# A graph network with attention on one core: shorter timetables for the attention of the last four pairs

## Chip, core and metric

The kernel runs on one core of a Trainium2 chip. The metric is the device time of one launch in microseconds (us): the median over several executions of the same program. The profile comes from one more execution; its span, from the first to the last instruction, is a little shorter than the timed figure.

## What is computed

There are 64 graphs of N = 256 nodes with D = 256 features each. A gated graph network (three layers, one GRU cell shared by all) is followed by one graph attention layer; each has a residual sum and a layer norm. Cut to what matters:

```python
A = (adj != 0)
h = x
for i in range(3):                       # gated graph network
    m = h @ weight[i]
    aggr = A^T @ m                       # over the nodes
    h = gru(aggr, h)                     # r, z sigmoid; n tanh; (1 - z) * n + z * h
v = layernorm(x + h)

wh = v @ W                               # attention
e = leaky_relu(s1[:, None] + s2[None, :])   # s1 = wh @ a1, s2 = wh @ a2
attn = softmax(where(adj > 0, e, -9e15))
out = layernorm(v + attn @ wh)
```

## The kernel before

**Tiling.** Two graphs make a pair, so 32 pairs (NP = 32) are worked off, numbered 0 to 31. A pair has K = 4 groups of 128 nodes; a tile of 128 partitions by 512 columns holds one half of the features of all its nodes, and fills one PSUM bank. The pool `psum` has eight banks; a product, a transpose or a projection takes the one that has been free for longest and waits until its last reader is done.

**Precision.** The products of the GRU split each operand in an upper part, a remainder and a difference (`pieces`, `upper`, `lower`, `cross`; H, L and D in the names), so that a gate product with a hidden and an input part is twelve passes of 128 by 512, one with a single part six. They are collected in two banks: `pga` (H and L parts) and `pgb` (D parts).

**Blocks.** Layer i of pair p is a block (p, i). The list `blocks` interleaves three pairs at different layers: it ends ... (31,0), (30,1), (29,2), (31,1), (30,2), (31,2). Each block is one call of `gates`, which issues the eight gate products of the two feature halves e = 0 and 1 (r, n, z, t each). After every six passes `product` calls `tick()`.

**The clock.** `tick()` advances a counter, and issues every step that is due. Everything else than the gate products hangs on that counter: `at(t, step)` puts a step into a heap, `run_due` takes out those whose time has come. A block has 12 ticks. So the instruction order of all five engines is written by this timetable at build time; at run time each engine works its own queue off in order, and waits by semaphore for the others.

**What hangs on it.** `front(p, i, t, pace)` prepares the next block (transposes `from_T`, splits, aggregation) in the ticks of the present one, by the tables `CLOSE` or `LOOSE`. In `gates`, the lags (2, 3, 5) or (4, 5, 10) say how many ticks after the last product of a half its tanh, its blend and its update of the state `hT` follow. The blend is done by GpSimd (two operations of 128 by 512, L394 and L395; the sum before the tanh is L404).

**Attention.** When the third block of a pair is done, `attention(p, clock)` puts its steps into the heap, with fixed offsets to that moment: reload the saved input (+5), `join` it with the state (+14), transpose back (+15), evacuate to `v` (+17), statistics of the layer norm (+23), its power and shift (+26, +28), projection by W (+31 to +34, each spread one tick later with the scale of the norm), the score rows (+36), the leaky ReLU (+37), mask (+38), row maximum (+39), exponentials (+46, +47), reciprocal and transposes of the weights (+52, +53), their evacuation (+54), product with `wh` (+57), sum (+58), second layer norm (+61 to +70) and store (+72). So the attention of a pair is spread over six blocks of other pairs. Pair 28 comes to its end about when the last block does. Pairs 29, 30 and 31 begin 36, 12 and 0 ticks before the end of the last block, and what is left of them is issued by the last loop, which has no gate products any more:

```python
    while pending:
        clock[0] = pending[0][0]
        run_due()
```

I call that part the tail. In it the three pairs' steps stand in the queues in the order of their due ticks.

**ScalarE's tables.** Exponentials (`exps`, L507) and sigmoids and tanh (`gate`, L386) need different activation tables, so a table load stands between them wherever the order changes from one kind to the other. In the middle of the kernel the exponentials of a pair stand at ticks 10 and 11 of a block, between the last sigmoid of that block and the first of the next: one load before them and one after.

Of the kernel before, what the change touches and what calls it, by code (L numbers as in the profile page):

```python
# [9 lines left out]
F32 = mybir.dt.float32  # L10
# [15 lines left out]
def kernel(  # L26
# [329 lines left out]
    def gates(p, i, lags):  # L356

        s = pairs[p]

        def product(dst, o, parts, bias=None):  # L360

            a, b = bank("pga"), bank("pgb")
            todo = [(a, w[k], m[k], d) for w, m in parts for k in (0, 1) for d in range(C)]
            ends = len(todo) - 1
            todo += [(b, w[2], m[2], d) for w, m in parts for d in range(C)]
            step = len(todo) // len(parts)
            for n, (pt, w, m, d) in enumerate(todo):
                nc.tensor.matmul(pt, w[:, d, o * P:(o + 1) * P], m[:, d, :],  # L368
                                 start=n in (0, ends + 1), stop=n in (ends, len(todo) - 1))
                if (n + 1) % step == 0 and n + 1 < len(todo):  # L370
                    tick()
            if bias is None:
                nc.scalar.activation(dst, a, AF.Copy, scale=1.0 + U)  # L373
            else:
                nc.scalar.activation(dst, a, AF.Identity, scale=1.0 + U, bias=bias)  # L375
            tick()
            nc.vector.scalar_tensor_tensor(dst, b, -1.0 / U, dst, op0=ALU.mult, op1=ALU.add)  # L377

        for e in range(C):
            nm = f"{p}_{i}_{e}"  # L380

            def temp(tag, bufs=2):
                return work.tile([P, GN], F32, tag=tag, name=f"{tag}_{nm}", bufs=bufs)

            def gate(dst, func, bias):
                nc.scalar.activation(dst, dst, func, bias=bias)  # L386

            hid, inp = (whh, s.hc), (wc[i], s.ag)
            bo = [b_sum[:, e:e + 1], b_sum[:, C + e:C + e + 1]]
            r, n, z, t = temp("r", 1), temp("n", 3), temp("z"), temp("t")  # L390
            h = s.hT[:, e, :]

            def blend(n=n, z=z, t=t, h=h):
                nc.gpsimd.tensor_sub(t, h, n)  # L394
                nc.gpsimd.tensor_mul(t, t, z)  # L395

            product(r, e, [hid, inp])
            after(1, lambda r=r, b=bo[0]: gate(r, AF.Sigmoid, b))
            product(n, 2 * C + e, [hid], bh[:, 2 * C + e:2 * C + e + 1])
            after(2, lambda r=r, n=n: nc.gpsimd.tensor_mul(n, n, r))  # L400
            product(z, C + e, [hid, inp])
            after(2, lambda z=z, b=bo[1]: gate(z, AF.Sigmoid, b))
            product(t, 2 * C + e, [inp])
            after(1, lambda n=n, t=t: nc.gpsimd.tensor_add(n, n, t))  # L404
            after(lags[0], lambda n=n, b=bi[:, 2 * C + e:2 * C + e + 1]: gate(n, AF.Tanh, b))
            after(lags[1], blend)
            after(lags[2], lambda n=n, t=t, h=h: nc.vector.tensor_add(h, t, n))

    def layer_norm(v, name, t, then=None):

        st = work.tile([P, K, nc.vector.BN_STATS_DIM], F32, tag="st_" + name[0], name=f"st_{name}")
        mv = work.tile([P, K, nc.vector.BN_AGGR_DIM], F32, tag="mv_" + name[0], name=f"mv_{name}")
        rs = work.tile([P, K], F32, tag="rs_" + name[0], name=f"rs_{name}")
        nm = work.tile([P, K], F32, tag="nmr_" + name[0], name=f"nmr_{name}")

        def stats(k):
            nc.vector.bn_stats(st[:, k, :], v[:, k // C, k % C, :])  # L417
            nc.vector.bn_aggr(mv[:, k, :], st[:, k, :])

        def power():  # L420
            nc.gpsimd.tensor_scalar(rs, mv[:, :, 1], EPS, None, op0=ALU.add)
            nc.gpsimd.tensor_tensor(rs, rs, half, ALU.pow)

        def shift():
            nc.vector.scalar_tensor_tensor(nm, mv[:, :, 0], -1.0, rs, op0=ALU.mult, op1=ALU.mult)

        def apply(k):
            vk = v[:, k // C, k % C, :]
            nc.scalar.activation(vk, vk, AF.Identity, scale=rs[:, k:k + 1], bias=nm[:, k:k + 1])  # L429

        for k in range(K):
            at(t[0] + k // 2, lambda k=k: stats(k))
        at(t[1], power)
        at(t[2], shift)
        for k in range(K):
            at(t[3] + k // 2, lambda k=k: apply(k))
        if then:
            at(t[3] + 2, then)
        return rs

    def attention(p, t):

        s = pairs[p]
        pts = {}

        def again():
            s.vT = room("vT", [P, C, GN], p)
            nc.sync.dma_start(s.vT, s.far)
        at(t + 5, again)
        at(t + 14, lambda: nc.vector.tensor_add(flat(s.vT), flat(s.vT), flat(s.hT)))  # L450

        def back(d):
            if d == 0:
                s.v = room("v", [P, G, C, D], p)
            pts[d] = from_T(s.vT, d)
        for d in range(C):
            at(t + 15 + d, lambda d=d: back(d))
            at(t + 17 + d, lambda d=d: nc.vector.tensor_copy(
                nodes(s.v, d), pts[d].rearrange("p (k n) -> p k n", k=K)))
        at(t + 18, lambda: setattr(s, "rs", layer_norm(s.v, f"a_{p}", (t + 23, t + 26, t + 28, t + 49))))  # L460

        def project(k):
            if k == 0:
                s.wh = room("wh", [P, G, C, D], p)
                s.s1 = work.tile([P, K], F32, tag="s1", name=f"s1_{p}")
                s.s2 = work.tile([P, K, P], F32, tag="hi0", name=f"s2_{p}", bufs=1)
            pts[k] = bank("pwh")
            for d in range(C):
                nc.tensor.matmul(pts[k][:, :D + 2], s.vT[:, d, k * P:(k + 1) * P], gw[:, d, :],  # L469
                                 start=(d == 0), stop=(d == C - 1))  # L470
# [8 lines left out]
                else:  # L479
                    nc.vector.tensor_scalar(dst, src, rs, None, op0=ALU.mult)  # L480
        for k in range(K):
            at(t + 31 + k, lambda k=k: project(k))
            at(t + 32 + k, lambda k=k: spread(k))

        def rows():
            pts[0] = bank("s2")
# [3 lines left out]
        def scores():  # L490
            s.sc = room("sc", [P, K, N], p)
            for k in range(K):
                nc.scalar.activation(s.sc[:, k, :], pts[0][:, (k // C) * N:(k // C + 1) * N], AF.Prelu,
                                     bias=s.s1[:, k:k + 1], alpha=ALPHA)
        at(t + 36, rows)
        at(t + 37, scores)

        s.nm = work.tile([P, K], F32, tag="nm", name=f"nm_{p}")
        s.sm = work.tile([P, K], F32, tag="sm", name=f"sm_{p}")

        def masked():
            nc.vector.copy_predicated(flat(s.sc), flat(s.mask), neg.to_broadcast([P, K * N]))  # L502
        at(t + 38, masked)
        at(t + 39, lambda: nc.vector.tensor_reduce(s.nm, s.sc, AX.X, ALU.max, negate=True))

        def exps(k):
            nc.scalar.activation(s.sc[:, k, :], s.sc[:, k, :], AF.Exp, bias=s.nm[:, k:k + 1],  # L507
                                 accum_out=s.sm[:, k:k + 1])
        for k in range(K):
            at(t + 46 + k // 2, lambda k=k: exps(k))  # L510
        at(t + 52, lambda: nc.vector.reciprocal(s.sm, s.sm))

        def weights_T(g):
            pts[g] = bank("pt")
# [16 lines left out]
                nc.vector.scalar_tensor_tensor(s.v[:, g, c, :], pts[g][:, c * D:(c + 1) * D], s.sm[:, k:k + 1],  # L531
                                               s.v[:, g, c, :], op0=ALU.mult, op1=ALU.add)
        for g in range(G):
            at(t + 53 + g, lambda g=g: weights_T(g))
            at(t + 54 + g, lambda g=g: nc.vector.tensor_copy(flat(s.sc[:, g * C:(g + 1) * C, :]), pts[g]))
            at(t + 57 + g, lambda g=g: combine(g))
            at(t + 58 + g, lambda g=g: add(g))
# [4 lines left out]
        at(t + 60, lambda: layer_norm(s.v, f"b_{p}", (t + 61, t + 64, t + 66, t + 70), store))  # L542


    CLOSE = (5, 5, 5, 7, 8, 8), (6, 6, 7)
    LOOSE = (2, 3, 4, 6, 7, 8), (5, 8, 10)


    blocks = []
# [28 lines left out]
    for n, (p, i) in enumerate(blocks):  # L578
        if n + 1 < len(blocks):
            np_, ni = blocks[n + 1]  # L580
            if ni == 0:
                after(1, lambda p=np_: begin(p))
            front(np_, ni, clock[0], CLOSE if n and np_ == blocks[n - 1][0] else LOOSE)
            if ni == 0:
                after(7, lambda p=np_: load_x(p + 1))
                after(16, lambda p=np_: masking(p))
                after(17, lambda p=np_: load_adj(p + 1))
        gates(p, i, (2, 3, 5) if n + 2 >= len(blocks) or blocks[n + 2][0] == p else (4, 5, 10))
        if i == L - 1:
            attention(p, clock[0])  # L590
    while pending:
        clock[0] = pending[0][0]
        run_due()
# [29 lines left out]
```

## Time and profile before

| | |
|---|---|
| time, median of 3 | 2256.81 us (2254.84 to 2256.81) |
| span of the profiled execution | 2254.2 us, mean granted TensorE clock 0.991 |
| TensorE (PE) busy | 2205.3 us, 98% |
| VectorE (DVE) busy | 1627.0 us, 72% |
| ScalarE (ACT) busy | 1494.6 us, 66% |
| GpSimd (POOL) busy | 1496.7 us, 66% |
| last gate matmul ends at | 2189.24 us |
| the tail, from there to the end of the span | 65.0 us |

The busy share of TensorE says that nearly the whole span is bound by it. The table's last two rows come from the chain of waits, which ends its list of gate products (L368) at 2188.78 us with a piece of 0.46 us. After it TensorE has work only now and then: the pieces of attention of three pairs, each waiting for the other engines.

### The profile page before, as it was taken

The page shows a single profiled execution, that of the slowest core. Times are in us where ns is not written, and L with a number is a line of the kernel's source. Part 1 is how long each engine was busy: PE and PEld are TensorE (multiplying, and loading weights), DVE is VectorE, ACT ScalarE, POOL GpSimd, SP SyncE. Part 2 cuts the span into 40 slices and gives each one's busy share as a digit, 9 for nine tenths or more (in the row PEclk, how much of TensorE's full clock was granted, in tenths as well). Part 3 has the DMA queues.
Part 4 walks back from the last instruction along what each step waited for, and adds up shares of the span by engine and source line. Part 5 has one row for each costly group of instructions (what it writes and reads, how often), then busy time and mean ns, then how long its engine had stood idle before and what let it go on. Part 6 is the DMA issues. An engine that isn't in the chain of part 4 may idle for free.

```text
span 2254.2 us, 31118 instructions
## 1 busy us (share of the span) xinstructions
PE 2205.3 (98%) x10980; PEld 1839.0 (82%) x10980; DVE 1627.0 (72%) x2856; ACT 1494.6 (66%) x2771; POOL 1496.7 (66%) x1084
## 2 busy tenths in 40 slices
PE   7999999999999999999999999999999999999985
PEld 5788888888888888888888888888888888888874
DVE  4767777777767777767777767777767777767775
ACT  4556667666667666667666677666677666677664
POOL 5777666676666676666667666667666667666661
PEclk9999999999999999999999999999999999999997
DMA  3001011100011101011101011101011101010000
GB/s 112 29 29 38 28 39 48 47 31 36 34 42 48 47 29 38 30 46 47 47 29 37 29 47 47 48 29 38 29 48 47 47 29 38 29 47 29 20 28 28
DMA packets 62650, 88.50 MB, mean 39 GB/s; under 512 B 2784, under 2 KB 54240, under 8 KB 62496
## 3 DMA queue, kind: packets, MB, share of 16 engines
q1 hardware_dynamic: 60704, 84.68, 10.7%
q8 instruction: 87, 1.43, 0.3%
q10 hardware_dynamic: 1616, 1.57, 0.2%
q14 instruction: 67, 0.55, 0.1%
q0 software_dynamic: 176, 0.27, 0.1%
HBM read 52.96 MB, written 33.55 MB: 38 GB/s over the span
## 4 chain that ended last, share of the span: by engine, by line
PE 95%; DVE 1%; ACT 1%; POOL 1%; issue 1%; DMA 1%; SPq 0%; POOLq 0%; ACTq 0%; DVEq 0%
PE pga L368 47%; PE pgb L368 23%; PE pa L339 8%; PE po L525 5%; PE pwh L469 5%; PE pt L274 4%; PE pt L268 1%; PE pt L517 1%; DMA adj<-in_adj_dram 1%; PE s L488 1%; PE pw L229 0%; ACT v L429 0%; DVE sc L502 0%; DVE st_b L417 0%; POOL wc2L_wc L145 0%
## 5 line engine op out<-in xcount | busy, mean ns | idle before, releaser
L394 POOL TENSOR_TENSOR t<-hT,n 128x512 f32<-128x512 f32 x192 | 255.0, 1328 | 534.3 <-ACT n L386 534.2
L368 PE MATMUL pga<-hH,whhH_whh 128*128 128x512 f32 x1152 | 397.4, 426 | 0.0
L368 PE MATMUL pgb<-hD,whhD_whh 128*128 128x512 f32 x1152 | 361.9, 395 | 0.3 <-DVE hD L134 0.3
L368 PE MATMUL pga<-hL,whhL_whh 128*128 128x512 f32 x1152 | 362.0, 395 | 0.0
L404 POOL TENSOR_TENSOR n<-n,t 128x512 f32<-128x512 f32 x192 | 251.8, 1311 | 114.2 <-DVE t L377 101.2
L377 DVE SCALAR_TENSOR_TENSOR r<-pgb,r 128x512 f32<-128x512 f32 x192 | 131.8, 686 | 254.0 <-PE pgb L368 188.5
L400 POOL TENSOR_TENSOR n<-n,r 128x512 f32<-128x512 f32 x192 | 306.2, 1595 | 0.6 <-DVE n L377 0.4
L395 POOL TENSOR_TENSOR t<-t,z 128x512 f32<-128x512 f32 x192 | 263.1, 1370 | 15.0
L368 PEld LDWEIGHTS pgb<-hD,whhD_whh 128*128 128x128 f32 x1152 | 216.3, 188 | 52.6 <-DVE hD L134 0.8
L368 PEld LDWEIGHTS pga<-hL,whhL_whh 128*128 128x128 f32 x1152 | 216.7, 188 | 51.4
L373 ACT ACTIVATE r<-pga 128x512 f32<-128x512 f32 x192 | 115.2, 600 | 216.0 <-PE pga L368 206.2
L375 ACT ACTIVATE n<-pga,bh 128x512 f32<-128x512 f32 x192 | 131.7, 686 | 164.6 <-PE pga L368 164.5
L131 POOL TENSOR_TENSOR hL<-hT,hH 128x1024 fp32r<-128x1024 f32 x96 | 230.6, 2402 | 7.1 <-ACT hH L128 7.1
L368 PEld LDWEIGHTS pga<-hH,whhH_whh 128*128 128x128 f32 x1152 | 193.9, 190 | 20.8
L339 PE MATMUL pa<-A,hi 128*128 128x256 f32 x768 | 200.4, 293 | 0.0
L373 ACT ACTIVATE z<-pga 128x512 f32<-128x512 f32 x192 | 114.7, 597 | 128.7 <-PE pga L368 128.7
L339 PE MATMUL pa<-A,lo 128*128 128x256 f32 x768 | 192.7, 283 | 4.3 <-POOL lo L131 4.3
L377 DVE SCALAR_TENSOR_TENSOR t<-pgb,t 128x512 f32<-128x512 f32 x192 | 131.8, 686 | 78.3 <-ACT t L373 72.3
L377 DVE SCALAR_TENSOR_TENSOR z<-pgb,z 128x512 f32<-128x512 f32 x192 | 131.9, 687 | 73.7 <-ACT z L373 60.9
L131 DVE TENSOR_TENSOR aL<-pa,aH 128x512 fp32r<-128x512 f32 x192 | 131.6, 685 | 55.4 <-ACT aH L128 55.4
L128 ACT ACTIVATE aH<-pa 128x512 fp32r<-128x512 f32 x192 | 115.1, 600 | 78.5 <-PE pa L339 78.5
L377 DVE SCALAR_TENSOR_TENSOR n<-pgb,n 128x512 f32<-128x512 f32 x192 | 131.8, 686 | 43.7 <-ACT n L375 39.3
(133 smaller groups left out, 5439.6 us busy)
## 6 DMA issues: line engine op xcount, KB each, us to landing
x<-in_x_dram SPq DMA_DIRECT2D x32, 512.0 KB, 4.0
adj<-in_adj_dram SPq DMA_DIRECT2D x32, 512.0 KB, 4.0
xT<-hT SPq DMA_DIRECT2D x32, 512.0 KB, 2.6
vT<-xT SPq DMA_DIRECT2D x32, 512.0 KB, 4.8
out_dram<-v SPq DMA_DIRECT2D x32, 512.0 KB, 2.9
w_n<-in_L_gnn_weight_dram ACTq DMA_DIRECT2D x3, 256.0 KB, 10.4
rows_hH<-in_L_gnn_w_hh_dram SPq DMA_DIRECT2D x1, 512.0 KB, 5.5
rows_aH<-in_L_gnn_w_ih_dram ACTq DMA_DIRECT2D x1, 512.0 KB, 6.0
```

The lines of the kernel that those rows point to most:

```text
L128: nc.scalar.activation(dst, src, AF.Copy, scale=1.0 - 2.0 ** -13)
L131: eng.tensor_sub(dst, src, hi.bitcast(F32))
L339: nc.tensor.matmul(pt[:, g * N:(g + 1) * N], h[:, g * C + c, :], s.A[:, g, c, :], start=(n == 0), stop=(n == len(todo) - 1))
L368: nc.tensor.matmul(pt, w[:, d, o * P:(o + 1) * P], m[:, d, :], start=n in (0, ends + 1), stop=n in (ends, len(todo) - 1))
L373: nc.scalar.activation(dst, a, AF.Copy, scale=1.0 + U)
L375: nc.scalar.activation(dst, a, AF.Identity, scale=1.0 + U, bias=bias)
L377: nc.vector.scalar_tensor_tensor(dst, b, -1.0 / U, dst, op0=ALU.mult, op1=ALU.add)
L394: nc.gpsimd.tensor_sub(t, h, n)
L395: nc.gpsimd.tensor_mul(t, t, z)
L400: after(2, lambda r=r, n=n: nc.gpsimd.tensor_mul(n, n, r))
L404: after(1, lambda n=n, t=t: nc.gpsimd.tensor_add(n, n, t))
L469: nc.tensor.matmul(pts[k][:, :D + 2], s.vT[:, d, k * P:(k + 1) * P], gw[:, d, :], start=(d == 0), stop=(d == C - 1))
```

## The change

The offsets become a table that depends on the pair. Pairs 0 to 27 keep theirs (`EVEN`). Pair 28 gets `BRISK` (the second layer norm's application at +54 instead of +70), pairs 29 to 31 get `FAST` (+33). The purpose is that less attention work is left when the gate products end. Three more parts belong to it:

- For these four pairs half of the evacuations of `v` and of the transposed weights move from VectorE to ScalarE (`copy`, even index).
- `s2`, which shared a buffer with the split of the next block (`hi0`), lies for these pairs in the buffer of the input `x`, which is free by then.
- The last block of pairs 29, 30 and 31 uses the short lags (2, 3, 5), and the last half of the last block does its three elementwise operations on VectorE instead of GpSimd.

```diff
+            add_by = nc.vector if (p, i, e) == (NP - 1, L - 1, C - 1) else nc.gpsimd
+
-            def blend(n=n, z=z, t=t, h=h):
-                nc.gpsimd.tensor_sub(t, h, n)
-                nc.gpsimd.tensor_mul(t, t, z)
+            def blend(n=n, z=z, t=t, h=h, eng=add_by):
+                eng.tensor_sub(t, h, n)
+                eng.tensor_mul(t, t, z)
...
-            after(1, lambda n=n, t=t: nc.gpsimd.tensor_add(n, n, t))
+            after(1, lambda n=n, t=t, eng=add_by: eng.tensor_add(n, n, t))
...
-    def attention(p, t):
+    def attention(p, t, pace):
...
+        T = {k: t + dt for k, dt in zip(
+            "again join back v stats power shift apply project rows scores mask max exp turn combine "
+            "stats2 power2 shift2 apply2".split(), pace)}
+
+        def copy(j, dst, src):
+            if pace is EVEN or j % 2:
+                nc.vector.tensor_copy(dst, src)
+            else:
+                nc.scalar.copy(dst, src)
...
-                s.s2 = work.tile([P, K, P], F32, tag="hi0", name=f"s2_{p}", bufs=1)
+                if pace is EVEN:
+                    s.s2 = work.tile([P, K, P], F32, tag="hi0", name=f"s2_{p}", bufs=1)
+                else:
+                    s2 = io.tile([P, G, C, D], F32, tag="x", name=f"s2_{p}")
+                    s.s2 = s2[:, 0].rearrange("p c (h n) -> p (c h) n", n=P)
...
+    EVEN = 5, 14, 15, 17, 23, 26, 28, 49, 31, 36, 37, 38, 39, 46, 53, 57, 61, 64, 66, 70
+    BRISK = 5, 14, 15, 17, 19, 21, 23, 32, 23, 28, 29, 30, 31, 33, 37, 41, 45, 48, 50, 54
+    FAST = 2, 5, 6, 7, 9, 10, 12, 22, 14, 18, 19, 20, 20, 22, 25, 27, 30, 31, 33, 33
...
-        gates(p, i, (2, 3, 5) if n + 2 >= len(blocks) or blocks[n + 2][0] == p else (4, 5, 10))
+        pace = EVEN if p < NP - 4 else BRISK if p < NP - 3 else FAST
+        close = n + 2 < len(blocks) and blocks[n + 2][0] == p or i == L - 1 and pace is FAST
+        gates(p, i, (2, 3, 5) if close else (4, 5, 10))
         if i == L - 1:
-            attention(p, clock[0])
+            attention(p, clock[0], pace)
```

The numbers of each table stand in the order of the names in `T`.

More of the change, by code (lines that the diff above doesn't have):

```diff
@@ L448, in again @@
             nc.sync.dma_start(s.vT, s.far)
-        at(t + 5, again)
-        at(t + 14, lambda: nc.vector.tensor_add(flat(s.vT), flat(s.vT), flat(s.hT)))
+        at(T["again"], again)
+        at(T["join"], lambda: nc.vector.tensor_add(flat(s.vT), flat(s.vT), flat(s.hT)))
         def back(d):
@@ L456, in attention, with norm @@
         for d in range(C):
[L457 to L460, printed above, removed]
+            at(T["back"] + d, lambda d=d: back(d))
+            at(T["v"] + d, lambda d=d: copy(d, nodes(s.v, d), pts[d].rearrange("p (k n) -> p k n", k=K)))
+        def norm():
+            s.rs = layer_norm(s.v, f"a_{p}", [T[k] for k in ("stats", "power", "shift", "apply")])
+        at(T["v"] + 1, norm)
         def project(k):
@@ L481, in attention @@
         for k in range(K):
-            at(t + 31 + k, lambda k=k: project(k))
-            at(t + 32 + k, lambda k=k: spread(k))
+            at(T["project"] + k, lambda k=k: project(k))
+            at(T["project"] + 1 + k, lambda k=k: spread(k))
         def rows():
@@ L494, in scores @@
                                      bias=s.s1[:, k:k + 1], alpha=ALPHA)
-        at(t + 36, rows)
-        at(t + 37, scores)
+        at(T["rows"], rows)
+        at(T["scores"], scores)
         s.nm = work.tile([P, K], F32, tag="nm", name=f"nm_{p}")
@@ L502, in masked @@
             nc.vector.copy_predicated(flat(s.sc), flat(s.mask), neg.to_broadcast([P, K * N]))
-        at(t + 38, masked)
-        at(t + 39, lambda: nc.vector.tensor_reduce(s.nm, s.sc, AX.X, ALU.max, negate=True))
+        at(T["mask"], masked)
+        at(T["max"], lambda: nc.vector.tensor_reduce(s.nm, s.sc, AX.X, ALU.max, negate=True))
         def exps(k):
@@ L509, in attention @@
         for k in range(K):
-            at(t + 46 + k // 2, lambda k=k: exps(k))
-        at(t + 52, lambda: nc.vector.reciprocal(s.sm, s.sm))
+            at(T["exp"] + k // 2, lambda k=k: exps(k))
+        at(T["turn"], lambda: nc.vector.reciprocal(s.sm, s.sm))
         def weights_T(g):
@@ L533, in attention @@
         for g in range(G):
[L534 to L537, printed above, removed]
+            at(T["turn"] + g, lambda g=g: weights_T(g))
+            at(T["turn"] + 1 + g, lambda g=g: copy(g, flat(s.sc[:, g * C:(g + 1) * C, :]), pts[g]))
+            at(T["combine"] + g, lambda g=g: combine(g))
+            at(T["combine"] + 1 + g, lambda g=g: add(g))
         def store():
@@ L541, in store @@
             del pairs[p]
-        at(t + 60, lambda: layer_norm(s.v, f"b_{p}", (t + 61, t + 64, t + 66, t + 70), store))
+        at(T["combine"] + 3, lambda: layer_norm(
+            s.v, f"b_{p}", [T[k + "2"] for k in ("stats", "power", "shift", "apply")], store))
     CLOSE = (5, 5, 5, 7, 8, 8), (6, 6, 7)
     LOOSE = (2, 3, 4, 6, 7, 8), (5, 8, 10)
+    EVEN = 5, 14, 15, 17, 23, 26, 28, 49, 31, 36, 37, 38, 39, 46, 53, 57, 61, 64, 66, 70
+    BRISK = 5, 14, 15, 17, 19, 21, 23, 32, 23, 28, 29, 30, 31, 33, 37, 41, 45, 48, 50, 54
+    FAST = 2, 5, 6, 7, 9, 10, 12, 22, 14, 18, 19, 20, 20, 22, 25, 27, 30, 31, 33, 33
     blocks = []
```

## The prediction, made before the changed kernel ran

> **What bounds the kernel now.** I read the page's first two parts, then the busy time in stretches of the last 65 us, then the waits of TensorE, last the timeline where ScalarE turns to the exponentials. First the page: busy time, and tenths of it in 40 slices.
>
> ```profile
> PE 2205.3 (98%) x10980; PEld 1839.0 (82%) x10980; DVE 1627.0 (72%) x2856; ACT 1494.6 (66%) x2771; POOL 1496.7 (66%) x1084
> PE   7999999999999999999999999999999999999985
> ACT  4556667666667666667666677666677666677664
> ```
>
> TensorE is full in every slice but the first and the last two. So work that is added to TensorE ahead of the tail costs its full duration, and so does every stall there; only the tail has room. The stretches of the tail (us; PE, PEld, DVE, ACT, POOL busy; granted clock; DMA):
>
> ```profile
> 2180.00:2190.00 10.00, 9.68 (x45) 7.77 (x43) 4.89 (x11) 7.43 (x17) 5.15 (x4) 1.00 0.05 17
> 2190.00:2200.00 10.00, 1.09 (x8) 0.86 (x8) 7.80 (x16) 7.50 (x19) 4.87 (x4) 0.75 0.28 88
> 2215.00:2220.00 5.00, 2.03 (x9) 1.12 (x7) 4.56 (x14) 2.11 (x8) 2.54 (x4) 0.89 0.00 0
> 2220.00:2225.00 5.00, 2.83 (x10) 1.80 (x10) 1.55 (x6) 5.00 (x17) 0.00 (x0) 0.50 0.08 29
> 2245.00:2250.00 5.00, 0.00 (x0) 0.00 (x0) 1.52 (x7) 1.80 (x4) 1.27 (x2) 0.62 0.00 0
> 2250.00:2255.00 5.00, 0.00 (x0) 0.00 (x0) 0.00 (x0) 0.27 (x1) 0.00 (x0) 0.50 0.30 105
> ```
>
> The reader should see that TensorE drops from full to a tenth at 2189.7 us, and that the work goes round between the engines. The waits of TensorE over the whole run (us in total, times, longest) show that ahead of the tail it hardly waits:
>
> ```profile
> PE po L525 <- DVE sc L535: 7.8, 2, 4.8
> PE s L488 <- DVE s L480: 2.7, 3, 2.2
> PE pgb L368 <- DVE hD L134: 0.3, 1, 0.3
> PE pt L274 <- DVE hT L407: 0.2, 1, 0.2
> ```
>
> Last, ScalarE in the timeline where pair 29 begins (start, duration). I choose it because the change moves exactly this group:
>
> ```profile
> 2139.62 0.71 ACT L386 ACTIVATE r<-r,b_sum 128x512 f32<-128x512 f32 x1
> ...
> 2140.36 1.28 ACT L507 ACT_TABLE_LOAD   x1
> ...
> 2142.65 0.58 ACT L373 ACTIVATE z<-pga 128x512 f32<-128x512 f32 x1
> ...
> 2144.11 0.58 ACT L373 ACTIVATE t<-pga 128x512 f32<-128x512 f32 x1
> ...
> 2145.70 1.28 ACT L386 ACT_TABLE_LOAD   x1
> ...
> 2147.62 0.58 ACT L373 ACTIVATE r<-pga 128x512 f32<-128x512 f32 x1
> ```
>
> ScalarE is without a gap from 2137.3 to 2150.9 here: one load, two exponentials (1.0 us), the evacuation of z, two exponentials, that of t, two applications of a norm (1.0 us), one load. The block ended at 2143.97, so z's bank came free 0.7 us before that, and TensorE did not feel it.
>
> **What the Trainium skill says.** "ScalarE: Activation LUTs", section "What ACT_TABLE_LOAD costs", gives 1283 ns for the load and as much again for a drain; the trace agrees on the load (1283 ns mean in each of its rows) and shows no drain, as the exponential starts 1.29 us after the load. The same page, "Table sets: the hidden batching unit", says that identity and copy are in every set; the trace agrees, as the norm applications stand between exponentials without a load. "PSUM — Partial Sum Buffer", "Specifications (TRN2)", has eight banks, which is the kernel's pool; that a late evacuation stops TensorE no run has shown yet. "TensorE: Matmul & The Clock Gate", "What's actually happening", says that an idle array runs at half clock until it has been busy some 3.4 us; the stretches agree (0.50 after idling, 0.98 to 1.00 later).
>
> **The change part by part.** The order of the changed program and its semaphore waits are known from its build; durations are from the rows of before, start to start where an engine is full: evacuation to or from 128x512 on ScalarE 0.5 to 0.6, sigmoid and tanh 0.63, two exponentials 1.0, two applications 1.0, DVE 128x512 0.61, mask and maximum together 2.6, four statistics 2.1, power on GpSimd 1.3.
>
> *Moved TensorE work.* Ahead of the end of the gates come from pair 29 the score rows (0.45), eight weight transposes (0.92) and the combination (3.46), from pair 30 eight transposes (0.92): +5.75 us, all on the bound engine.
>
> *Pair 28 (BRISK), exponentials at +33 and +34, ticks 9 and 10 of block (29,2).* There the sigmoid of r stands between the two halves, and pair 27's last norm (+70) falls on the same ticks. ScalarE's queue becomes: evacuate r, apply 28, aH, tanh, evacuate n, load, two exponentials, apply 28, load, sigmoid r, load, two exponentials, apply 27, evacuate z, apply 27, evacuate t, load, sigmoid z, evacuate the next r, copy of the weights. A pass takes 0.233 us (2 in 0.47). With the block's end on TensorE as 0, r's first bank is ready at -6.5 (0.9 of r, 1.4 of n, 2.8 of z and 1.4 of t still to come); the sum to the evacuation of z is 0.48+1.0+0.5+0.61+0.57+1.29+1.0+1.0+1.29+0.63+1.29+1.0+1.0+0.6 = 12.3, so it ends at +5.8 instead of before 0; t follows at 7.3, the next r at 9.7. TensorE needs these banks at 3.7 (front transpose: 2.8 of r and 0.92 of weight transposes), 5.1 and 6.1 (next z). The last waits longest: 9.7 - 6.1 = a stall of 3.6 us. Behind it in TensorE's queue are all later products, so nothing hides it. Less is possible only if r's evacuation starts earlier; 3 to 5.
>
> *Pair 29 (FAST) in block (30,2).* Rows (+18) are due in the same tick as the last spread they read. DVE reaches it late: it has eight statistics (4.2 us) at the end of (31,1), the power on GpSimd waits for these and the gates' sum for the power, then tanh, two spreads and hi0 on ScalarE, lo0 and z on DVE. I get the last s2 at 1.3 us after TensorE is there: +1.3 (0 to 3). Then mask and maximum stand ahead of the splits of block (31,2) on DVE, which delays the sigmoid of r, behind which the exponentials wait. The copy of the first weights, now on ScalarE, stands behind the second table load, a sigmoid and an evacuation: it ends 7.7 us after the block, while the combination is due at 5.1: +2.6 (1 to 5).
>
> *Blend, lags, s2's buffer, copies.* The lags let the states of 29 and 30 be ready for the joins, at 15 and 70 us of a walk in which TensorE comes at 18 and 70: nothing. The buffer only removes a wait. The copies on ScalarE are priced above.
>
> Stalls: 3.6 + 1.3 + 2.6 = 7.5; the gates end at 2189.24 + 5.75 + 7.5 = 2202.5.
>
> *The tail*, from that end as 0, pairs 30 and 31 only. GpSimd's product n*r comes late (power of pair 30 stands ahead): 2.5. Sum 0.7, tanh 0.7, two operations on VectorE 1.3: 5.2 (GpSimd took 2.3 and 1.3 for these). A spread 0.8, state 0.65, join 1.15, last s2 of pair 30 0.45: 8.25. Rows 0.35, scores 1.6, mask and maximum 2.6: 12.8. Load 1.3, exponentials and applications 4.0, copy 0.6: 18.7. Then the projection of 31 and the combination of 30 take turns on TensorE, 6 us at full clock, 7.7 with the first part at half: 26.4; spread 0.6, rows 0.35, scores 1.6, mask and maximum behind the statistics of 30, 3.0: 32.0. Exponentials with three pairs of applications, pair 30's ahead of them: 6.2; copy 0.6: 38.8. Combination 5.4 as before: 44.2. From there the end is as before, 2254.2 - 2243.36 = 10.84 (sum, statistics, power, shift, application, store): 55.0 us, against 65.0. So the tail gives 10.0, and 5.75 + 7.5 are paid for it.
>
> Span 2202.5 + 55.0 = 2257.5, or 3.3 more than before; time 2256.8 + 3.3 = 2260.1.
>
> **The rivals.** *A, the gain stays:* the stalls do not come, because the queues have the slack that 66% busy ScalarE and 72% busy DVE suggest and the banks are enough. For it: TensorE never waited on a ScalarE evacuation before. Against: ScalarE is without a gap where the group stands now, and the new order adds two loads and two applications there. Stalls of 1, tail of 54.5: 2256.8 + 5.75 + 1 - 10.5 = 2253.0, or faster. *B, the queues jam more:* DVE's 128x1024 operations took up to 2.3 us beside GpSimd (mean 1.64 for the hD row), each late state delays the next block, and ScalarE's backlog is passed on. Stalls of 15: 2256.8 + 5.75 + 15 - 10 = 2267.5, slower. Against it: pair 30 meets a block without front work. *C, the tail is not shortened:* the DMA that reloads pair 31's input stands behind pair 29's store and lands later than the join at 6.65; before it took 3.2 to 4.6 us to land. Issued at 1.2, it lands near 6: at most 2 us, 2262.
>
> **How the numbers follow.** My forecast (stalls 4 to 11, results 2256.6 to 2263.6) gets 0.55, A 0.20, B 0.20, C 0.05. 0.2% is 4.5 us, so "within" is 2252.3 to 2261.3. Of the forecast's 0.55, 0.33 lies within and 0.22 above; of A 0.11 below and 0.09 within; B is above; of C 0.01 within, 0.04 above. I move 0.04 from slower to faster, because every duration was read from another place of the trace. That makes 0.15, 0.43, 0.42. The range leaves out the better part of A and the worst of B: 2252.3 to 2267.5.
>
> **What would show it.** Four table loads more on ScalarE than before (61 to 65); TensorE waits of 3 to 5 us on evacuations about 80 us before the gates' end, and of 2 to 3 us on ScalarE's copy 20 us before it; last gate matmul near 2202; span after it near 55. If the gates end at 2196, A is right. If the tail is 50 or less, I mis-sized its chain.

## The result and the profile after

| | before | after |
|---|---|---|
| time, median | 2255.97 us (2254.84 to 2256.81) | 2265.99 us (2264.05 to 2268.2) |
| ratio, 95% interval | | 1.0045 [1.0028, 1.0062] |
| span of the profiled execution | 2254.2 us | 2263.5 us |
| end of the gates | 2189.1 us | 2205.8 us |
| the tail | 65.1 us | 57.7 us |
| table loads on ScalarE | 61 | 65 |

The end of the gates is counted here and below to the start of the instruction that follows the last gate matmul on TensorE; that matmul's own end is some 0.15 us later (2189.24 us before). Tails are differences of rounded figures and may be off by 0.1 us.

The changed kernel is slower by 0.45%, 10.0 us by the medians. The tail did become 7.4 us shorter, but the gates end 16.7 us later. The page of the kernel after, in the rows shown of before:

```profile
PE 2208.0 (98%) x10980; PEld 1837.6 (81%) x10980; DVE 1629.1 (72%) x2851; ACT 1502.8 (66%) x2783; POOL 1490.4 (66%) x1081
PE   7999999999999999999999999999999999999984
ACT  4556667666667666667666677666667666667664
```

There is little to see in it: TensorE has the same 10980 instructions, and a slice of 57 us is too coarse for stalls of 2 us. The busy time in stretches of the kernel after (us; PE, PEld, DVE, ACT, POOL busy; granted clock; DMA) shows them. Before, no stretch of ten between 2080 and 2180 had less than 9.77 us of PE:

```profile
2110.00:2120.00 10.00, 10.00 (x55) 8.48 (x54) 7.66 (x12) 8.10 (x16) 7.52 (x5) 1.00 0.01 2
2120.00:2130.00 10.00, 8.09 (x38) 5.96 (x36) 5.01 (x6) 9.91 (x19) 4.20 (x3) 1.00 0.00 1
2130.00:2140.00 10.00, 8.62 (x40) 6.76 (x41) 6.04 (x9) 8.87 (x16) 5.09 (x4) 1.00 0.33 105
...
2160.00:2170.00 10.00, 7.72 (x41) 6.32 (x40) 7.46 (x13) 6.94 (x16) 5.05 (x4) 1.00 0.01 2
...
2180.00:2190.00 10.00, 6.57 (x30) 4.38 (x29) 3.84 (x8) 9.96 (x22) 3.64 (x3) 1.00 0.00 0
```

Where TensorE falls to 8.09 and 6.57, ScalarE stands at 9.91 and 9.96: there it is the engine that is waited for. From 2160 to 2170 us it is not; there TensorE waits for VectorE. The waits of TensorE from 2090 us to the gates' end name them (before had a single one of 0.2 us there):

```profile
PE po L542 <- ACT sc L455: 2.5, 1, 2.5
PE s L505 <- DVE s L497: 2.3, 1, 2.3
PE pt L534 <- ACT sc L524: 2.1, 5, 1.0
PE pga L368 <- ACT r L373: 1.1, 1, 1.1
PE pt L274 <- ACT z L373: 0.9, 1, 0.9
```

The first is pair 29's combination waiting for ScalarE's copy, the second pair 29's rows. Of the third, 1.2 us come from pair 28's exponentials and 0.9 us from pair 29's; the last two stand behind pair 28's exponentials. ScalarE's timeline at pair 28's site (start, duration; the block ends at 2123.82 on TensorE):

```profile
2120.84 1.28 ACT L524 ACT_TABLE_LOAD   x1
...
2124.24 1.28 ACT L386 ACT_TABLE_LOAD   x1
2125.53 0.72 ACT L386 ACTIVATE r<-r,b_sum 128x512 f32<-128x512 f32 x1
2126.28 1.28 ACT L524 ACT_TABLE_LOAD   x1
...
2129.55 0.57 ACT L373 ACTIVATE z<-pga 128x512 f32<-128x512 f32 x1
...
2131.61 1.28 ACT L386 ACT_TABLE_LOAD   x1
...
2133.53 0.58 ACT L373 ACTIVATE r<-pga 128x512 f32<-128x512 f32 x1
```

Four loads within 12 us; two of them are there only because one sigmoid stands between the two halves of the exponentials. The evacuation of z ends 6.3 us after the block, that of the next r 10.3 us. TensorE's timeline beside it (in brackets: idle time, and who ended it):

```profile
2128.22 0.33 PE L534 MATMUL pt<-ident,sc 128*128 128x128 f32 x1 [1.01 <-ACT sc L524]
...
2130.18 0.66 PE L274 MATMUL pt<-ident,hT 128*128 128x128 f32 x4 [0.92 <-ACT z L373]
...
2134.16 0.73 PE L368 MATMUL pga<-hH,whhH_whh 128*128 128x512 f32 x2 [1.14 <-ACT r L373]
```

The product of z starts 10.34 us after the block. In e7 below, where nothing waits at this place, it starts 6.38 us after it, behind the same work: 4.0 us are lost here. (The prediction counted 6.1 us of work ahead of it; the 4.3 us in the expectation of e1 come from such a count.) Of the 3.3 us of waiting at this place 0.92 and 1.14 are for the evacuations of z and r. These belong to the gates and have nothing to do with attention, but they stand behind it in ScalarE's queue.

### The profile page after: what moved, and what is told of

Its sections match the earlier page's. It is cut to its first block, busy times and chain, and to the rows that moved or that the text cites. A ratio compares the mean times of both kernels' runs of the same rounds, so it can differ in the third digit from the quotient of the medians.

```text
span 2263.5 us, 31147 instructions
## 1 busy us (share of the span) xinstructions
PE 2208.0 (98%) x10980; PEld 1837.6 (81%) x10980; DVE 1629.1 (72%) x2851; ACT 1502.8 (66%) x2783; POOL 1490.4 (66%) x1081
## 3 DMA queue, kind: packets, MB, share of 16 engines
q8 instruction: 87, 1.43, 0.3%
## 4 chain that ended last, share of the span: by engine, by line
PE 93%; DVE 2%; ACT 2%; POOL 1%; DMA 1%; issue 1%; SPq 0%; POOLq 0%; ACTq 0%; DVEq 0%
PE pga L368 46%; PE pgb L368 23%; PE pa L339 8%; PE po L542 5%; PE pwh L486 5%; PE pt L274 4%; PE pt L268 1%; PE pt L534 1%; PE s L505 1%; DMA adj<-in_adj_dram 1%; ACT v L431 1%; PE pw L229 0%; ACT sc L524 0%; DVE hD L134 0%; DVE st_b L419 0%
## 5 line engine op out<-in xcount | busy, mean ns | idle before, releaser
L402 POOL TENSOR_TENSOR n<-n,r 128x512 f32<-128x512 f32 x192 | 305.7, 1592 | 4.7 <-ACT r L386 3.0
```

## The experiments

Two theories of the time before the gates' end. The first: a few instructions stand in the wrong place of a queue, and each can be moved. The second: ScalarE and VectorE have too much to do in these blocks, so that a wait that is removed comes back elsewhere. For the tail, likewise: it is set by the order in which the pairs stand in the queues, or by the amount of work in it. "Gates" below is the time from the start of block (31,0) to the last gate matmul. It is counted from there because that start differs by up to 4 us between profiled executions, although nothing before it was changed. Each run has one profiled execution. The ratios are to executions of the kernel before that were timed beside the run, with medians from 2255.26 to 2256.74 us.

| run | gates, us | tail, us | time, us | ratio to before, 95% |
|---|---|---|---|---|
| before | 132.9 | 65.1 | 2255.97 | |
| after | 149.8 | 57.7 | 2265.99 | 1.0045 [1.0028, 1.0062] |
| e1 exponentials of 28 | 148.4 | 57.4 | 2264.26 | 1.0039 [1.0025, 1.0053] |
| e2 copies on VectorE | 147.2 | 57.8 | 2263.23 | 1.0036 [1.0023, 1.0049] |
| e3 rows of 29 | 150.0 | 56.9 | 2264.86 | 1.0045 [1.0033, 1.0058] |
| e4 blend on GpSimd | 149.8 | 58.8 | 2267.79 | 1.0054 [1.0041, 1.0066] |
| e5 only 30, 31 short | 135.2 | 62.7 | 2255.35 | 0.9998 [0.9990, 1.0007] |
| e6 only 28, 29 short | 149.9 | 59.2 | 2268.44 | 1.0054 [1.0041, 1.0067] |
| e7 e1 to e3 together | 142.8 | 56.5 | 2257.89 | 1.0006 [0.9998, 1.0014] |
| e8 blend, with long lags | 132.9 | 65.7 | 2256.30 | 1.0003 [0.9994, 1.0011] |
| e9 new order in the tail | 142.8 | 47.2 | 2247.48 | 0.9963 [0.9948, 0.9977] |
| e10 pair 29 once more | 142.6 | 46.9 | 2248.64 | 0.9962 [0.9949, 0.9975] |
| e11 e9 without 28, 29 | 135.0 | 48.1 | 2239.15 | 0.9924 [0.9911, 0.9937] |
| e12 e11, old order | 135.0 | 59.3 | 2251.14 | 0.9978 [0.9972, 0.9985] |

### One wait at a time

**e1: pair 28's exponentials one tick later**, so that the sigmoid of r no longer splits them.

```diff
-    BRISK = 5, 14, 15, 17, 19, 21, 23, 32, 23, 28, 29, 30, 31, 33, 37, 41, 45, 48, 50, 54
+    BRISK = 5, 14, 15, 17, 19, 21, 23, 32, 23, 28, 29, 30, 31, 34, 37, 41, 45, 48, 50, 54
```

> Pair 28's exponentials one tick later (34 and 35 instead of 33 and 34), so that no sigmoid stands between its two halves. Stall theory (the time is lost where ScalarE's order delays the release of PSUM banks): two table loads (2.6 us) go, the wait of TensorE at the end of block (29,2) falls from 4.3 us to about 1, the gates end at 2202.5 instead of 2205.8, the tail stays at 57.7, time 2262.7. Backlog theory (ScalarE and VectorE are simply too full in these blocks, and a wait that is taken away at one place comes back at the next): the table loads go, but the gates' end moves by less than 1 us, time 2265 to 2266.

Measured: block (31,1) took 26.41 us instead of 29.25, so 2.84 were gained where the wait was; the loads fell to 63. But (30,2) and (31,2) together took 54.20 instead of 52.76, and 1.44 were lost again. At first that looked like a wait handed on. It is not one: the list of waits there is the same, that of pair 29's combination is 2.52 us in both. What differs is the combination after it. TensorE's timeline of e1:

```profile
2187.20 3.42 PE L542 MATMUL po<-wh,sc 128*128 128x256 f32 x8 [2.52 <-ACT sc L455]
```

and of the kernel after:

```profile
2188.56 1.99 PE L542 MATMUL po<-wh,sc 128*128 128x256 f32 x8 [2.52 <-ACT sc L455]
```

The same eight matmuls take 1.43 us longer. The stretches of e1 say why (last three columns: granted clock, DMA share and GB/s):

```profile
2183.30:2186.71 3.41, 1.38 (x6) 0.77 (x5) 0.78 (x3) 3.38 (x6) 1.26 (x1) 1.00 0.00 0
2186.71:2190.12 3.41, 2.92 (x7) 2.38 (x8) 1.98 (x3) 2.24 (x4) 2.20 (x2) 0.50 0.00 0
```

During the wait of 2.5 us the clock went to half, for 3.41 us; in the profiled execution of the kernel after it did not (the last section says when it does). So what came back was the price of a wait that was still there, not a new one. The time, 2264.26 us, lies between the two theories.

**e2: all copies on VectorE again.**

```diff
         def copy(j, dst, src):
-            if pace is EVEN or j % 2:
+            if True:
                 nc.vector.tensor_copy(dst, src)
```

> All evacuations of v and of the transposed weights on VectorE again, for all pairs. Stall theory: in block (31,2) the first weights of pair 29 no longer stand behind a table load, a sigmoid and an evacuation on ScalarE, so the combination's wait falls from 2.7 to about 1.1 us; in the tail each copy comes about 1 us sooner, because on ScalarE it stood behind four norm applications: gates end 2204.2, tail 55.7, time 2262.4. Balance theory (two engines share the evacuations, so taking one away costs): VectorE is then late, gates' end the same or later, tail longer by 1 to 2 us, time 2266 to 2268.

Measured: the wait of the combination fell from 2.5 to 1.0 us, that of the next r at pair 28 (1.1) went away, and the gates took 2.7 us less, more than expected. The tail did not move (57.8 against 57.7), where 2 us less had been expected. So sharing these copies is a loss: the Trainium skill's "TensorEngine Tiling (Array Packing)", section "PSUM Bottleneck", advises both engines for evacuation, and here VectorE alone is better: in these stretches ScalarE is busy 9.9 of 10 us, and the same wait for a copy is 1.0 us on VectorE instead of 2.5.

**e3: pair 29's rows one tick later.**

```diff
+    LATER = 2, 5, 6, 7, 9, 10, 12, 22, 14, 19, 20, 21, 21, 22, 25, 27, 30, 31, 33, 33
...
-        pace = EVEN if p < NP - 4 else BRISK if p < NP - 3 else FAST
+        pace = EVEN if p < NP - 4 else BRISK if p < NP - 3 else LATER if p < NP - 2 else FAST
```

> Pair 29 alone: score rows, scores, mask and maximum one tick later (19, 20, 21, 21). Stall theory: TensorE's wait of 2.4 us for the last spread falls to about 0.8 us, and the gates end near 2204.2; time 2264.3. Backlog theory: VectorE is as late with the mask and maximum, the splits of block (31,2) and the sigmoid of r follow as late as before, and the wait comes back at the exponentials' transposes; gates end 2205.8, time 2266.

Measured: the rows' wait of 2.3 us is gone, one of 1.1 us for pair 31's state on VectorE (L409) has come, and the gates' end is where it was. By itself that speaks for the second theory. But the clock was at half twice in this execution, 0.53 and 0.61 in the two stretches from 2130 on, 0.54 and 0.61 from 2188 on, and PE was busy 2.8 us more in these three blocks than in the kernel after, with the same instructions. Block (30,2), where the rows stand, took 24.77 us instead of 25.97; block (31,2), where the clock was at half for the second time, took 1.3 us more. So the gain was covered, not absent.

**e7: the three together** tells the theories apart.

> The whole change with three edits together: BRISK's exponentials one tick later, all copies on VectorE, pair 29's rows, scores and mask one tick later. Order theory (each wait is an instruction queued at the wrong place, so the gains add and what came back in the later blocks does not): gates' end 141 to 143 us after block (31,0) starts, tail 57 to 58, time 2257 to 2259. Backlog theory (VectorE and ScalarE have too much to do in these blocks and another wait takes the place): no better than the copies alone, gates' end near 147, time 2262 to 2264.

Measured: gates 142.8, a gain of 7.0 us, and 8.1 us in the time. That is what the first theory expected. Singly the three showed 1.4, 2.7 and nothing, in sum 4.1. Without the half clock e1 is 2.8 and e3 1.4 (1.58 of extra PE time in its last two blocks, against a length of 52.90 for 52.76), in sum with e2 6.9, about what they give together. The single blocks show the same without that working: block (31,1) lost 2.84 us in e1, 1.13 in e2 and 3.98 in e7; block (30,2) lost 1.20 in e3 and in e7. The waits of TensorE in e7 from 2090 us to the gates' end, with the clock at 1.00 throughout:

```profile
PE pt L274 <- DVE hT L409: 1.1, 1, 1.1
PE po L542 <- DVE sc L453: 1.0, 1, 1.0
PE pt L534 <- ACT sc L524: 0.6, 3, 0.3
```

Of the 11.1 us that the kernel after lost beside the moved work, 4.2 are left; the list names 2.7 of them. With this the change can't be told from the kernel before (ratio 1.0006 [0.9998, 1.0014]).

**e10** goes for the two longer of these waits, on the tables of e9: pair 29's statistics and its combination one tick later.

```diff
-    LATER = 2, 5, 6, 7, 9, 10, 12, 22, 14, 19, 20, 21, 21, 22, 25, 27, 30, 31, 33, 33
+    LATER = 2, 5, 6, 7, 10, 11, 13, 22, 14, 19, 20, 21, 21, 22, 25, 28, 31, 32, 33, 34
```

> The same, with pair 29's statistics one tick later and its combination one tick later. Order theory: the 1.0 us wait of the combination for its copies and the 1.1 us of the transposes for hT are gone, gates' end 141 us after block (31,0) starts, time 1.5 to 2 below the run before it. Backlog theory: VectorE hands the wait on to another instruction, and the time is within 0.5 of it.

Measured: the combination's wait is gone, the one for L409 is 1.3 now and one of 0.8 is new; the gates gained 0.2 us and the time nothing (2246.64 to 2248.93 against 2246.99 to 2249.33). Here the second theory is nearer: what is left is handed on.

### What makes the tail short

**e5 and e6** are the two halves of the change.

```diff
-        pace = EVEN if p < NP - 4 else BRISK if p < NP - 3 else FAST
+        pace = EVEN if p < NP - 2 else FAST                                                    (e5)
+        pace = EVEN if p < NP - 4 else BRISK if p < NP - 3 else FAST if p < NP - 2 else EVEN   (e6)
```

> Pairs 28 and 29 keep the even timetable, pairs 30 and 31 take FAST. Theory 1 (the tail is short because the last two pairs have short timetables and their copies are shared): gates' end near 2190 to 2192 (133 us after block (31,0) starts, plus 0.9 for pair 30's transposes and at most 1 of waits), tail 57 to 59, time 2250 to 2252, faster than before. Theory 2 (the tail is short because pair 29's combination and norm no longer stand in it): gates' end the same, tail 63 to 66, time 2256 to 2259.

> The other half: BRISK for pair 28 and FAST for pair 29, the even timetable for pairs 30 and 31. Theory 1: gates' end 147 to 149 us after block (31,0) starts (all but pair 30's 0.9 and the block (31,2) waits), tail 63 to 65, time 2271 to 2274. Theory 2: the same gates' end, tail 57 to 59, time 2264 to 2267.

Measured: the short tables of pairs 30 and 31 alone shorten the tail by 2.4 us and cost 2.2 at the gates, in sum nothing. The short tables of pairs 28 and 29, which move pair 29's part out of the tail, shorten it by 5.9 and cost 17.0 at the gates, pair 28's waits among them. So the second theory is nearer: most of the tail's gain came with pair 29's leaving. It hardly pays for itself: even without any wait, pair 29's moved TensorE work of 4.83 us (5.75 without pair 30's 0.92) would take up most of the 5.9. One thing parts e6 from a clean half: `close` asks for `FAST`, so the last blocks of pairs 30 and 31 get the long lags (4, 5, 10) in it, where the kernel before has the short ones. How much of e6's tail that is was not measured.

**e4 and e8: the blend.** e4 gives the last blend back to GpSimd. e8 is the kernel before with this part, and, for the same reason as in e6, with the long lags in the last blocks of pairs 30 and 31.

```diff
-            add_by = nc.vector if (p, i, e) == (NP - 1, L - 1, C - 1) else nc.gpsimd
+            add_by = nc.gpsimd                                         (e4)
...
-        pace = EVEN if p < NP - 4 else BRISK if p < NP - 3 else FAST
+        pace = EVEN                                                    (e8)
```

> The last half's sum and blend on GpSimd as before the change. The three operations took 2.1 us on VectorE; on GpSimd 1.3 each, 3.9 or up to 4.9 us. If the state of pair 31 is on the path that sets the end of the tail (my walk): tail 59.5 to 60.5 instead of 57.7, time 2268 to 2269. If pair 30's attention covers it: tail 57.7, time 2266. The gates' end stays at 2205.8 in both.

> The kernel before with one part of the change: the last blend, and the addition of t to n ahead of it, on VectorE. If the blend is worth the 1.1 us that taking it away cost: tail 64, time 2254.2 to 2254.6. If another wait hides it in the longer tail: tail 65, time 2255.3, the same as before.

Measured: in the changed kernel it is worth 1.1 us of tail in the one profiled execution of each; the timed executions of the two overlap (2266.05 to 2269.04 us, 2264.05 to 2268.2). In e8 nothing is gained, the tail is 65.7. That alone doesn't show that the blend is worth nothing there, as e8 has the long lags and pair 31's state is done later in it than before: 9.6 us after the gates' end, where it was 8.0. The trace of before shows it without e8 (VectorE):

```profile
2196.35 0.69 DVE L407 TENSOR_TENSOR hT<-t,n 128x512 f32<-128x512 f32 x1 [0.79 <-POOL t L395]
...
2199.82 1.19 DVE L450 TENSOR_TENSOR vT<-vT,hT 128x1024 f32<-128x1024 f32 x1
```

Pair 31's state is done at 2197.0, but its join (L450) starts only at 2199.8, behind pair 30's statistics in VectorE's queue. An earlier state would have waited longer. So the part can help only where pair 31's state is what the tail waits for.

**e9: another order in the tail.** The tail of the kernel after on TensorE:

```profile
2215.86 1.92 PE L274 MATMUL pt<-ident,vT 128*128 128x128 f32 x8
2222.39 1.39 PE L534 MATMUL pt<-ident,sc 128*128 128x128 f32 x4 [4.62 <-ACT sc L524]
...
2225.54 1.93 PE L486 MATMUL pwh<-gw,vT 128*128 128x258 f32 x4
...
2231.94 1.91 PE L486 MATMUL pwh<-gw,vT 128*128 128x258 f32 x8
...
2234.41 0.33 PE L505 MATMUL s<-ident,s 128*128 128x128 f32 x1 [0.24 <-DVE s L497]
2241.11 1.39 PE L534 MATMUL pt<-ident,sc 128*128 128x128 f32 x4 [6.37 <-ACT sc L524]
...
2246.00 6.59 PE L542 MATMUL po<-wh,sc 128*128 128x256 f32 x16 [0.55 <-ACT sc L455]
```

Pair 31 is transposed at 2217.8, and its projections (L486) need nothing but that. Yet they stand behind pair 30's weights (L534), which wait for pair 30's exponentials; TensorE is idle for 4.62 us meanwhile, and pair 31's last row (L505) is only done at 2234.7. e9 takes the three edits of e7 and gives pairs 30 and 31 tables of their own, which let pair 31 go ahead:

```diff
+    NEXT = 2, 5, 6, 7, 9, 12, 13, 27, 14, 19, 20, 22, 22, 24, 26, 29, 34, 35, 37, 37
+    LAST = 2, 5, 6, 7, 8, 9, 10, 18, 9, 13, 14, 15, 15, 16, 18, 20, 23, 24, 26, 26
...
+        pace = EVEN if p < NP - 4 else (BRISK, LATER, NEXT, LAST)[p - NP + 4]
```

> The three mends, and tables of their own for pairs 30 and 31: pair 31's projections straight after its transposes and ahead of pair 30's weights, its statistics ahead of pair 30's mask and maximum, pair 30's power and first norm later, its combination after pair 31's rows. Theory 1 (the tail is a chain of one pair waiting behind the other in each engine's queue): gates' end 143 us after block (31,0) starts as with the three mends, tail 49 to 52, time 2251 to 2253, faster than before. Theory 2 (the tail is set by how much VectorE and ScalarE have to do there, whatever the order): tail 54 to 56, time 2256 to 2258.

Measured: tail 47.2, 9.2 us less than in e7 with the same gates' end; time 2247.48, faster than the kernel before. It is more than the order theory expected.

**e11: the new order, and pair 29 left in the tail.** The copies stay on VectorE. Pair 28 is on the even table again, pair 29 nearly so, with its old lags.

```diff
+    HALF = 5, 14, 15, 17, 23, 26, 28, 40, 31, 36, 37, 38, 39, 46, 50, 53, 56, 58, 59, 59
...
-        pace = EVEN if p < NP - 4 else (BRISK, LATER, NEXT, LAST)[p - NP + 4]
+        pace = EVEN if p < NP - 4 else (EVEN, HALF, NEXT, LAST)[p - NP + 4]
```

With this table three pairs need `sm` at once, so it gets a third buffer.

> The new tables for pairs 30 and 31, but pair 28 on the even timetable and pair 29 too up to its maximum, so that its weights, combination and last norm stay in the tail (its weights 3 ticks earlier there than before). If pair 29's part fits into idle time of the tail once the two pairs stand in a good order: gates' end 135 to 136 us after block (31,0) starts, tail 52 to 54, time 2247 to 2250, the fastest of all. If it stands in their way, as with the short tables: tail 57 to 60, time 2252 to 2255.

Measured: the fastest of all, 2239.15 us, ratio 0.9924 [0.9911, 0.9937], and the tail is shorter than expected, 48.1. With pair 29's weights, combination and norm in it the tail is 0.9 us longer than e9's; moved ahead of the gates' end, together with pair 28's short table, they cost 7.8 there (142.8 against 135.0). TensorE in the tail of e11, the gates having ended at 2189.0:

```profile
2199.74 1.06 PE L274 MATMUL pt<-ident,vT 128*128 128x128 f32 x4
2200.59 5.15 PE L486 MATMUL pwh<-gw,vT 128*128 128x258 f32 x16
...
2207.65 0.55 PE L505 MATMUL s<-ident,s 128*128 128x128 f32 x3 [1.41 <-ACT s L495]
...
2210.75 3.72 PE L542 MATMUL po<-wh,sc 128*128 128x256 f32 x16 [0.24 <-DVE sc L453]
2214.68 3.72 PE L542 MATMUL po<-wh,sc 128*128 128x256 f32 x16 [0.21 <-DVE sc L453]
...
2219.97 3.72 PE L542 MATMUL po<-wh,sc 128*128 128x256 f32 x16 [0.69 <-DVE sc L453]
```

From pair 31's transposes to its last row it takes 7.4 us instead of 17.0 (2200.8 to 2208.2; 2217.8 to 2234.7). The three combinations run at full clock, 3.72 us each; in the kernel after the last one began after an idle stretch and took 6.59.

**e12** gives FAST back to pairs 30 and 31 in e11, to tell the order from pair 29's earlier end and the copies.

```diff
-        pace = EVEN if p < NP - 4 else (EVEN, HALF, NEXT, LAST)[p - NP + 4]
+        pace = EVEN if p < NP - 4 else (EVEN, HALF, FAST, FAST)[p - NP + 4]
```

> The fastest kernel with FAST given back to pairs 30 and 31, so that only pair 29's earlier end and the copies on VectorE tell it from the run with short tables for 30 and 31 alone. If the order of pairs 30 and 31 against each other made the tail short: gates' end 135 us after block (31,0) starts, tail 60 to 63, time 2252 to 2255. If pair 29's earlier end made it short: tail 48 to 52, time 2239 to 2243.

Measured: tail 59.3, time 2251.14. Of the 14.6 us by which e11's tail is shorter than e5's, 11.2 are the order of pairs 30 and 31; 3.4 are pair 29's earlier end and the copies, which were not parted. The longest entry in TensorE's waits of e12, from 2191 us on:

```profile
PE pt L534 <- ACT sc L524: 12.7, 4, 7.1
```

and the same entry of e11, from 2188 us on:

```profile
PE pt L534 <- ACT sc L524: 0.2, 1, 0.2
```

The longest wait that e11 has left there is one of 4.8 us, for pair 31's join (L461) on VectorE.

## Why the prediction was right, and what it missed

It gave 2260.1 us in a range of 2252.3 to 2267.5, and "within 0.2%" a hair before "slower". The time, 2265.99, lies in the range, on the slower side. The mechanism was the one that the runs showed; two terms of the sum were too small. The number fits less well than it looks: the sum gave a rise of 3.3 us, counted from 2256.8, and the rise was 10.0; the time lies outside the forecast's own 2256.6 to 2263.6. That the range holds it is owed to the share that rival B had in it, whose rise of 10.7 came nearer.

- *Moved TensorE work, 5.75 us at full cost:* the full cost is right, the price was low. e7, which still moves it and has few waits, ends its gates 9.9 us later than before, of which 2.7 are named waits; that leaves 7.2 for it. TensorE's busy time from the start of block (31,0) to the gates' end agrees: 140.0 us in e7, 132.7 before. Why it is 1.5 us more than its price is not shown.
- *Four more table loads:* 65, as predicted; e1 took two away.
- *Pair 28's stall of 3.6 at the next r's bank:* the place and the chain of three waits are right, the size was 4.0. The sum to the evacuation of z gave +5.8 where it ended at +6.3, the next r +9.7 where it ended at +10.3.
- *Pair 29's rows, 1.3 (0 to 3):* 2.3. That VectorE is late was right. On its way to the rows the update of pair 31's state (L409) took 1.76 us beside GpSimd (last section), where 0.66 to 0.69 is usual, and that is about the size of the miss; what the eight statistics did to it was not tested.
- *Pair 29's combination, 2.6 (1 to 5):* 2.5 at the start of the combination, and 0.9 more at its weights' transposes, which I had left out.
- *The step that failed by size is "Stalls: 3.6 + 1.3 + 2.6 = 7.5"*: 11.1 were lost in its place (149.8 - 132.9 - 5.75, rounded). The listed waits make up 8.9 of that. The rest is busy time: TensorE was busy 140.8 us between the start of block (31,0) and the gates' end, 8.1 more than before, where the moved work was priced at 5.75. The gates so end at 2205.8 instead of 2202.5.
- *The tail, 55.0:* 57.7. Blend done at 6.7 instead of 5.2, maximum of pair 30 at 14.5 instead of 12.8, the last combination 6.6 us instead of 5.4, as the clock was at half for most of it. The half clock after an idle stretch had been reckoned with for the projections of 31; for the combination the prediction took the 5.4 us of before.
- *Blend, lags, buffer: nothing.* Right for the gates. For the tail the blend was worth 1.1 us, where the prediction's own durations (2.3 and 1.3 on GpSimd, 1.3 for both on VectorE) give 2.3; in the tail of before it would have been worth nothing, as pair 31's join there waits for its turn and not for the state.
- *Rival A* (a gain stays, stalls of 1) was wrong as to the stalls. *Rival B* (stalls of 15) had the direction that the miss took: late states, and VectorE slow beside GpSimd. *Rival C* did not come: the join was not late for its load.
- Readings: the ScalarE lines from 2139.62 on are pair 28's exponentials in block (31,1); pair 29's attention had begun at 2123.9. That block ended at 2143.50 and not at 2143.97, so z's bank came free 0.3 us ahead of it and not 0.7. Neither changes the sum.
- What no rival said: the tail had 9 to 11 us to give by its order alone (e9 against e7, e11 against e12), without any work moved out of it.

It stays open how the timed executions are divided between full and half clock after the waits; each profile shows one execution.

## What to carry to other kernels

Where one engine is full and has idle time only at the end, its work belongs into that idle time: taking it out pays only if the end is really set by it, and here it paid back 5.9 us for 17.0 (e6), and in the good order of the tail 0.9 for 7.8 (e9 against e11). Before moving work out of a tail, look at the order in it: an instruction that has all its inputs but stands behind one that waits is time for nothing, and here a new order gave 9 to 11 us. When single mends seem to be given back, try them together before concluding that the queue is full, and compare the clock as well as the waits.

## What the runs showed that was not expected

**A wait of 2.5 us can halve the clock, and need not.** The Trainium skill's "TensorE: Matmul & The Clock Gate", section "What's actually happening", speaks of a window of some 3.4 us that runs freely, and the section "HAM oscillation — how this bites in real kernels" of idle gaps longer than that. The traces agree on the window: in each of them all changes of clock lie whole multiples of 3.41 us apart. They don't agree on the gap. From 100 us to the gates' end the clock went to half five times in all the traces, once in e1 and twice each in e3 and e6, and each time TensorE had been busy for 1.30 to 1.38 us of the 3.41 before. A window with 1.51 us (e2, 2165.24 to 2168.65) left it at full, and so did all with more. (In the tails the limit is less sharp: the clock also fell after three windows with 1.6 to 1.8 us.) The wait of 2.52 us in the kernel after falls into two windows:

```profile
2183.58:2186.99 3.41, 2.28 (x11) 1.47 (x10) 0.99 (x3) 3.38 (x7) 0.61 (x1) 1.00 0.00 0
2186.99:2190.40 3.41, 1.84 (x9) 1.63 (x10) 1.95 (x3) 3.33 (x6) 1.85 (x2) 1.00 0.00 0
```

In e1 most of the same wait lies in one, with TensorE busy 1.38 us (shown there), and the clock fell. In e3 two waits of 1.0 and 0.9 us in one window were enough (1.32 us busy from 2126.72 to 2130.13). So what counts here is not the length of a wait but how much of it falls into one window. The extra cost in e1 was 1.4 us, more than half of the wait itself.

**VectorE beside GpSimd.** The operation for hD (128 by 1024) takes 1.21 us at its fastest. After pair 29's rows:

```profile
2170.78 3.29 DVE L134 SCALAR_TENSOR_TENSOR hD<-hH,hT 128x1024 fp32r<-128x1024 f32 x1
```

with GpSimd's subtraction beside it:

```profile
2170.58 2.41 POOL L131 TENSOR_TENSOR hL<-hT,hH 128x1024 fp32r<-128x1024 f32 x1 [4.62 <-ACT hH L128]
```

It ends 1.1 us after GpSimd's does, as if it had only begun then. That is what "SBUF — State Buffer", section "🔬 SBUF: two separate sides", says of the port pair that the two share: who starts first holds it for the whole instruction. The update of pair 31's state, which stands ahead of the spreads that pair 29's rows wait for, behaves alike. GpSimd's L402 ran beside it from 2164.69 to 2165.97, and it ends 0.55 us after that:

```profile
2164.76 1.76 DVE L409 TENSOR_TENSOR hT<-t,n 128x512 f32<-128x512 f32 x1 [0.69 <-POOL t L397]
```

The tiny shift of a norm (L427, 128 by 4) fits too: 0.15 us at its fastest, and 1.25 us at 2157.44, where an operation of GpSimd (L402) had started 0.06 us earlier.
